# When lane X may begin an output: from the fifth step of a block instead of the third

## The chip, the cores and the metric

The kernel runs on one NeuronCore of a Trainium2 chip. The metric is the device time of one launch in microseconds (us). The kernel before took 5182.59 us as the median of three runs, which lay between 5178.62 and 5191.08 us.

The engines are named as in the profile: PE is TensorE's matmuls, PEld its weight loads, DVE is VectorE, ACT is ScalarE, POOL is GpSimd, SP is SyncE, which here issues all DMAs of the main loop.

## What is computed

An image batch of shape (4, 128, 64, 64) goes through two layers. Cut to what matters:

```python
# layer 0, on x of shape (B=4, C=128, 64, 64), with a residual
xn = layernorm(group_norm(x))                      # over channels
h  = gelu(layernorm(depthwise_conv3x3(xn)))        # then a 1x1 convolution fc2
y  = layernorm(xn + fc2(h))
m  = mamba(y in 4 chunks of 32 channels) + skip * y   # selective scan over 4096 pixels
x  = x + proj(layernorm(xn + m))
# layer 1, on tokens t of shape (4, 4096, 128)
t = t + attention(layernorm(t))                    # 4 heads of 32, all 4096 keys
t = t + top2_of_8_experts(layernorm(t))            # softmax router, 128x128 experts
```

Inside `mamba`, each of 64 channels and 16 states per chunk runs `h = dA * h + dBu` over the pixels, and `y = sum over states of h * C`. Everything is fp32.

## The kernel before

**Blocks and units.** The 4096 pixels of a batch are cut into 8 blocks of 512, so there are 32 blocks, numbered here 0 to 31 (batch = number divided by 8). A block is scanned in 16 units: two halves of the channels, times eight pairs of states. One unit is one `TENSOR_TENSOR_SCAN` of 128 x 1025 on DVE, with a multiply before it (`h<-rows,du`) and one after it (`hc<-rows,h`), eight transposing matmuls that sum `hc` over the states (`y<-ident,hc`), and two exponentials on ACT (`da`).

**Steps.** One loop (`while` after line 1340) runs over steps, called `slot` in the code. Two steps make a unit, so a block is 32 steps and the 32 blocks end at `END` = 1024. A step's place in its block is `slot % 32`; "the third step" is the one with number 2. In each step the program issues, in this order: the loads of rows for a later unit, the decays of the next unit (ACT), in even steps the multiply before the scan, then the second half-step of lane X, one group of attention (4 matmuls `sc`, 2 exponentials `pT`), the scan (even) or the multiply after it (odd), the first half-step of lane Y, the summing transposes, the second half-step of lane Y, the eight matmuls `av` of the attention group of the step before, and the first half-step of lane X. Every engine keeps this order: `queued` (line 406) ties each instruction to the one before it on its engine, which is also why nearly all lines of the profile read L406.

**Lanes.** All work that is neither scan nor attention goes through two lanes, each a queue of tasks written as generators. One half-step is one `yield`. A lane runs one task to its end before it takes the next.

- Lane Y prepares blocks: `in` (the inputs of one channel half: projections, Silu, softplus; 3 steps), `y0` (first norm of a later block; 5 steps), `xn` (convolution, gelu, fc2 and two norms for the next block; 13 steps). In most blocks the order is `in` (from step 3), `y0` (from 6), `xn` (from 11; its convolution taps, 1.5 us of DVE per step, in steps 11 to 15), `in` of the next block (from 24). In blocks 14, 22 and 30 there is no `y0` after the first `in`, so `xn` runs from step 6.
- Lane X finishes blocks. `closed(b, i)` (line 793; 18 half-steps, 9 steps) takes a scanned block through the output projection, the last norm, and the attention's keys, queries and values. When its last half-step is done, `("closed", b, i)` is in `done`. `finished(b, qb, lane)` (line 1032; 30 half-steps, 15 steps; the task is called `out`) takes a block of 512 queries whose attention is complete through the projection (`aT`, `acc`), the router with its top-2 choice (`pr`, `top1`, `pick1`, `both`), and the experts (`share`, `res`). Its half-steps 0 to 19 are loads, projection and router; the eight experts come in half-steps 20 to 28.

**How lane X picks.** When the second channel half of a block is summed, in step 3 of the next block, `summed_up` (line 778) puts `closed` at the front of lane X's queue. An `out` task is put at the end of the queue when its attention is complete. `advance` (line 1254) takes the first task of the queue, with one condition for `out`: before step `END + 4` it is begun only in a window of steps of the block. A task that runs is never interrupted: where an `out` was begun in step 2, `closed` of that block waits until it ends in step 17.

**Attention.** A batch has 256 groups: for each of 4 pairs of query blocks and 4 heads, 32 key tiles in groups of two. `RUNS` (line 903) orders them so that parts whose blocks are closed come first; `ready` (line 908) checks this. The generator gives one group per step, or none where the next part's blocks aren't closed yet. Lane Y takes `out` tasks too once its own queue is empty, from step `END` on, but never a `closed`.

**Buffers.** Each lane has one PSUM bank for its work (`ps_X`, `ps_Y`); a matmul group is written in the first half-step and read in the second. Lane Y's `in` also uses `ps_X` inside a step. `rows` has 4 buffers, `hc` 2, `pT` 4, `sc` 2, lane X's temporaries 6.

Of the kernel before, what the change touches and what calls it, by code (L numbers as in the profile page):

```python
# [24 lines left out]
NST = 16  # L25
# [11 lines left out]
def conv_mamba_attn_moe_kernel(ctx: ExitStack, tc: tile.TileContext, t: dict):  # L37
# [1216 lines left out]
    def advance(lane, second):  # L1254

        if inside[lane] != second:
            return False
        while True:
            if lane not in running:

                tasks = lanes[lane] if lanes[lane] or slot < END else lanes["X"]
                if tasks and lane == "Y" and tasks[0][0][0] == "closed":
                    return False
                if not tasks or not all(k in done for k in tasks[0][2]):
                    return False

                if (
                    tasks[0][0][0] == "out" and slot < END + 4
                    and not 2 <= slot % (2 * NST) < NST + 2
                ):  # L1270
                    return False
                key, stages, _ = tasks.popleft()
                running[lane] = key, stages(lane) if callable(stages) else stages
            key, stages = running[lane]
            try:
                next(stages)
                inside[lane] = not second
                return True
            except StopIteration:
                assert not second  # L1280
                done.add(key)
                del running[lane]

    def until(key):
        while key not in done:
            flush()
            count = len(done)
            moved = [
                advance(*half) for half in (("X", True), ("Y", False), ("Y", True), ("X", False))
            ]  # L1290
            assert any(moved) or len(done) > count, key
            if ("y0", *blocks[1]) in done:
                next(weights, None)
# [49 lines left out]
    h_of, slot = {}, 0  # L1343
# [18 lines left out]
    while (  # L1362
# [16 lines left out]
        if summing:  # L1379
            summed_up(*summing)  # L1380
            summing = None
        advance("X", True)
        group = next(groups, None)
        if group:
# [3 lines left out]
        if unit and odd:  # L1388
            hc = read(h, rows.pop((at, 1)))
            late = 2 * (unit[3] == 0)  # L1390
            due.append((slot + 1 + late, unit, 0, hc[:, 0, :], False))
            due.append((slot + 2, unit, 1, hc[:, 1, :], ends(unit)))
        advance("Y", False)
        while closing and closing[0][0] <= slot:
            summing = turned_back(*closing.popleft()[1:])
# [133 lines left out]
```

## Time and profile before

| what | value |
|---|---|
| median of three runs | 5182.59 us |
| the profiled execution's own time | 5183.13 us |
| its span, first to last instruction | 5180.9 us |
| start of the first scan | 77.8 us |
| start of the last scan (unit 511) | 4570.1 us |
| closing of the last block begins (DVE `cm<-xn,w_skip`) | 4653.8 us |
| first `out`'s loads are issued | 1299.2 us |
| `acc<-ps_X,acc`: outputs in lane X | 27 |
| `acc<-ps_Y,acc`: outputs in lane Y, the first at 4594.5 us | 5 |
| scan on DVE, 512 times | 2353 ns each |
| exponential `pT` on ACT, 2048 times | 1022 ns each |
| table load on ACT, 319 times | 1283 ns each |

How to read it: the start of the scan of unit 16k is the start of block k on DVE, so a block's length is the time from one such scan to the sixteenth after it. Blocks 11, 13, 19, 21 and 27 last 143.5, 142.2, 143.6, 143.5 and 143.5 us. Blocks 14, 22 and 30 last 159.6, 163.4 and 158.9 us. Blocks 7 and 17, in which lane X only closes a block, last 133.5 and 138.9 us. After the last block only attention and outputs remain, some 600 us.

In lists of waits and groups, a name like `ps_X<-ident,bothX` is output, then inputs; "PE ps_X <- DVE bothX" is a wait of PE, before a matmul into `ps_X`, for DVE's write of `bothX`.

### The profile page before, as it was taken

What the parts mean: (1) busy time and instruction counts of PE and PEld (TensorE: products, weight loads), DVE (VectorE), ACT (ScalarE), POOL (GpSimd) and SP (SyncE); (2) the same over time, 40 slices, a digit from 0 to 9 for tenths busy, and PEclk for the clock granted to TensorE, in tenths of its full rate; (3) what the DMA queues carried; (4) which work ended last, traced back from release to release, by engine and by line L of the source; (5) the groups of instructions that cost most, each with busy time, mean ns of one, the idle gap of its engine ahead of it and who ended that gap; (6) DMA issues with size and microseconds to landing.
All of it is one profiled execution on the core that took longest, in us unless ns stands there. A gap on an engine that the chain in (4) does not pass through costs nothing.

```text
span 5180.9 us, 62597 instructions
## 1 busy us (share of the span) xinstructions
PE 4710.1 (91%) x20684; PEld 2321.9 (45%) x20684; DVE 3835.8 (74%) x5780; ACT 3745.7 (72%) x5700; POOL 423.1 (8%) x483
## 2 busy tenths in 40 slices
PE   4567898999999998899999999999999999999997
PEld 2334444444444444444444444444444444443443
DVE  6987767877778887878788887888788877751332
ACT  4556777787787787688888787788777787656543
POOL 1111111100000000101000000000000001000000
PEclk7778999999999999899999999999999999999998
DMA  3556667677666766767766766777766666754542
GB/s 127 183 186 212 205 212 253 233 239 243 229 224 225 239 227 234 242 230 258 252 228 227 238 229 231 258 231 255 265 227 233 221 230 221 262 179 156 184 134 72
DMA packets 451693, 1131.70 MB, mean 218 GB/s; under 512 B 51858, under 2 KB 135331, under 8 KB 451363
## 3 DMA queue, kind: packets, MB, share of 16 engines
q1 hardware_dynamic: 447296, 1125.96, 64.3%
q8 instruction: 166, 2.72, 0.2%
q10 hardware_dynamic: 4066, 1.67, 0.1%
q14 instruction: 165, 1.34, 0.1%
HBM read 967.22 MB, written 143.39 MB: 214 GB/s over the span
## 4 chain that ended last, share of the span: by engine, by line
PE 59%; DVE 19%; ACT 10%; DMA 6%; issue 4%; POOL 2%; SPq 1%; DVEq 0%; ACTq 0%; POOLq 0%
PE av L406 25%; PE sc L406 14%; PE ps_X L406 9%; DVE h L406 6%; PE ps_Y L406 6%; PE y L406 5%; ACT pT L406 3%; ACT L406 2%; DVE hc L406 2%; DMA ks<-kd 2%; ACT xt L406 1%; DVE stX L406 1%; DVE du L406 1%; DMA rows<-bcd 1%; DVE cm L406 1%
## 5 line engine op out<-in xcount | busy, mean ns | idle before, releaser
L406 ACT ACTIVATE pT<-sc 128x1024 f32<-128x1024 f32 x2048 | 1984.3, 1022 | 934.3 <-PE sc L406 932.8
L406 PE MATMUL av<-pT,v 128*64 128x512 f32 x8192 | 2002.8, 610 | 10.8 <-DVE avs L406 10.8
L406 PE MATMUL sc<-qs,ks 128*128 128x512 f32 x4096 | 1302.7, 437 | 75.9 <-ACT pT L406 39.4
L406 DVE TENSOR_TENSOR_SCAN h<-da,state,h 128x1025 f32<-128x1025 f32 x512 | 1204.5, 2353 | 96.6 <-ACT h L406 62.8
L406 PEld LDWEIGHTS sc<-qs,ks 128*128 128x128 f32 x4096 | 703.1, 190 | 812.7 <-ACT pT L406 273.2
L406 PEld LDWEIGHTS av<-pT,v 128*64 128x64 f32 x8192 | 500.4, 137 | 845.7 <-issue 816.7
L406 ACT ACTIVATE da<-delta,amat 128x512 f32<-128x512 f32 x1024 | 742.9, 730 | 1.9
L406 PE MATMUL y<-ident,hc 128*128 128x128 f32 x4096 | 626.2, 284 | 64.6 <-DVE hc L406 64.6
L406 DVE TENSOR_TENSOR hc<-rows,h 128x1024 f32<-128x1024 f32 x512 | 624.6, 1220 | 15.3 <-PE y L406 5.4
L406 DVE TENSOR_TENSOR h<-rows,du 128x1024 f32<-128x1024 f32 x512 | 623.9, 1218 | 13.0 <-DMA rows<-bcd 8.5
L406 PEld LDWEIGHTS y<-ident,hc 128*128 128x128 f32 x4096 | 524.2, 147 | 229.0 <-issue 80.8
L406 ACT ACT_TABLE_LOAD x319 | 409.3, 1283 | 19.5 <-DVE zs L406 14.3
L406 POOL TENSOR_TENSOR rsX<-rsX,mhalf 128x4 f32<-128x4 f32 x92 | 203.7, 2214 | 2504.4 <-DVE rsX L406 2420.4
L406 POOL TENSOR_TENSOR rsY<-rsY,mhalf 128x4 f32<-128x4 f32 x100 | 130.7, 1307 | 2072.5 <-DVE shiftY L406 1561.5
L406 DVE TENSOR_TENSOR avs<-av,prev 128x512 f32<-128x512 f32 x96 | 66.2, 689 | 256.7 <-PE av L406 235.0
L406 PE MATMUL ps_X<-share,w_ew 128*128 128x512 f32 x432 | 213.9, 617 | 9.1 <-DVE share L406 8.8
L406 ACT ACTIVATE xt<-ps_Y,shiftY,rsY 128x128 f32<-128x128 f32 x380 | 143.6, 468 | 81.7 <-POOL shiftY L406 73.8
L406 DVE TENSOR_TENSOR share<-share,xf 128x1024 f32<-128x1024 f32 x128 | 156.0, 1219 | 16.5 <-DMA share<-sharesX 11.7
L406 ACT COPY state<-h 128x2 f32<-128x2 f32 x448 | 88.8, 198 | 92.0 <-DVE h L406 92.0
L406 DVE SCALAR_TENSOR_TENSOR cm<-y,w_fc1w,cm 128x512 f32<-128x512 f32 x195 | 145.1, 744 | 8.0 <-ACT y L406 4.5
L406 PE MATMUL ps_Y<-pairs,inxc 128*128 128x512 f32 x256 | 132.6, 643 | 15.5 <-DMA pairs<-xn 9.9
L406 PEld LDWEIGHTS ps_X<-share,w_ew 128*128 128x128 f32 x432 | 73.2, 189 | 147.0 <-issue 97.1
(248 smaller groups left out, 3437.2 us busy)
## 6 DMA issues: line engine op xcount, KB each, us to landing
rows<-bcd SPq DMA_DIRECT2D x1024, 512.0 KB
ks<-kd SPq DMA_DIRECT2D x192, 512.0 KB
qs<-qd SPq DMA_DIRECT2D x161, 512.0 KB
share<-sharesX SPq DMA_DIRECT2D x108, 512.0 KB
v<-vd SPq DMA_DIRECT2D x192, 256.0 KB
ks<-kd SPq DMA_DIRECT2D x128, 256.0 KB
avd<-avs SPq DMA_DIRECT2D x96, 256.0 KB
prev<-avd SPq DMA_DIRECT2D x96, 256.0 KB
```

The lines of the kernel that those rows point to most:

```text
L406: return lambda *args, **kw: queued(op(*args, **kw))
```

## The change

```diff
                 if (
                     tasks[0][0][0] == "out" and slot < END + 4
-                    and not 2 <= slot % (2 * NST) < NST + 2
+                    and not 4 <= slot % (2 * NST) < 18
                 ):
                     return False
```

`NST` is 16, so the upper end is 18 in both. The window in which an `out` may begin was steps 2 to 17 of a block and is now steps 4 to 17. `closed` enters the queue in step 3. Nothing is added or removed: the same tasks with the same instructions run, in another order.

## The prediction

> **What bounds the kernel now.** I read the page first: engine shares, then the slices.
>
> ```profile
> PE 4710.1 (91%) x20684; PEld 2321.9 (45%) x20684; DVE 3835.8 (74%) x5780; ACT 3745.7 (72%) x5700; POOL 423.1 (8%) x483
> ...
> PE   4567898999999998899999999999999999999997
> ...
> PEclk7778999999999999899999999999999999999998
> ```
>
> PE is full from the fifth slice to the last; the idle time of its start, before attention has data, is outside the change. So I took PE's idle time block by block. Busy time by windows, each from a block's first scan to the next block's (us, then busy time by engine, PEclk, DMA share, GB/s):
>
> ```profile
> 943.20:1076.70 133.50, 126.94 (x586) 61.89 (x585) 104.46 (x136) 113.15 (x163) 15.48 (x19) 1.00 0.64 213
> 2394.60:2533.50 138.90, 131.44 (x601) 63.96 (x599) 109.75 (x144) 114.32 (x175) 12.12 (x13) 0.99 0.76 259
> 2966.60:3110.10 143.50, 140.05 (x641) 69.47 (x640) 117.74 (x176) 117.70 (x183) 11.68 (x15) 1.00 0.70 241
> 3855.10:3998.60 143.50, 140.05 (x641) 69.48 (x640) 117.75 (x176) 116.86 (x181) 11.60 (x14) 1.00 0.67 222
> 1662.20:1804.20 142.00, 127.53 (x574) 65.59 (x572) 118.11 (x177) 108.12 (x172) 11.60 (x14) 0.95 0.71 236
> 1946.40:2106.10 159.70, 133.39 (x560) 68.14 (x559) 128.20 (x198) 101.63 (x160) 15.11 (x11) 0.86 0.75 256
> 3110.10:3273.50 163.40, 150.90 (x664) 74.33 (x664) 128.60 (x197) 118.26 (x180) 12.95 (x15) 0.96 0.74 259
> 4677.00:4792.00 115.00, 115.00 (x464) 45.15 (x460) 9.23 (x13) 72.28 (x76) 0.00 (x0) 1.00 0.46 157
> ```
>
> These are blocks 7, 17, 21, 27, 12, 14, 22, and a stretch of attention alone at the end. Blocks 21 and 27, with an output begun in step 2 and the closing after it, are PE's work (140.05) plus 3.45 us of idle. Blocks 7 and 17, which close in step 3 and have no output, have less work and more idle: 6.6 and 7.5 us. Blocks 12 and 14 lack attention groups in 5 and 8 steps and PE's clock falls. The end is PE alone.
>
> PE's waits in block 7, then in block 21 (total us, times, longest):
>
> ```profile
> PE sc L406 <- ACT pT L406: 2.7, 6, 1.8
> PE ps_Y L406 <- DVE gn L406: 2.1, 1, 2.1
> PE ps_Y L406 <- ACT xt L406: 1.3, 1, 1.3
> PE ps_Y L406 <- ACT g L406: 0.4, 1, 0.4
> ```
> ```profile
> PE ps_X L406 <- DVE bothX L406: 1.9, 1, 1.9
> PE sc L406 <- ACT pT L406: 0.9, 4, 0.4
> PE ps_X L406 <- DVE lo L406: 0.7, 1, 0.7
> ```
>
> The reader is to see that the order in lane X decides which waits a block has. The 2.1 us for `gn` stands in blocks 5, 7, 8, 9 and 17 alike, all that close first: DVE gets to `gn` behind `tt` and the moments of `closed`.
>
> [...]
>
> **The steps, counted from the code.** `closed` takes 9 steps, `out` 15. Before: `out` 2 to 17, `closed` 17 to 26. After: `closed` 3 to 12, `out` 12 to 27 (12 is inside the window). This turns over blocks 10 to 16 and 18 to 31; block 9's output begins in step 16 in both. 22 outputs begin before `END` in both; 22 in lane X plus 5 there in the tail is the 27 of the profile.
>
> Closing 14 steps sooner feeds attention sooner. Taking `ready` step by step, no group is ready in 5 steps of block 12 and 8 of block 14; after the change in 1 and 0. The other steps without a group are the same. So 891 groups, not 879, are done before `END`; 133, not 145, remain, and the loop has 1182 steps, not 1194. The last closing moves from steps 1041-1050 to 1027-1036, but attention doesn't lack groups there, so this alone gives nothing.
>
> **Part 1, twelve groups out of the tail.** In the stretch of attention alone the chain has `av` x8 of 1.87 us and `sc` x4 of 1.12: 2.99 a group. 12 x 2.99 = -35.9.
>
> **Part 2, the steps that they fill.** Blocks 12 and 13 take 142.0 + 142.2 = 284.2 with the holes; two full ones take 2 x 143.5 = 287.0: +2.8. Blocks 14 and 15 take 301.8; the full pair 22 and 23 takes 163.4 + 139.2 = 302.6: +0.8. Together +3.6: PE's idle time and slow clock are traded for work. Net of parts 1 and 2: -32.3.
>
> **Part 3, the order in the 17 ordinary blocks** (10 to 13, 15, 16, 18 to 21, 23 to 29). PE's work is the same 140.05, so a block changes by its waits and its clock. The waits of the new order, in order of steps, from the blocks that already close first:
> - before `closed` the wait for `pT`: 0.2 in both.
> - `gn` in steps 6 to 7: 2.1. Upstream nothing differs from block 7. Ends 1.5 and 2.1.
> - `pT` after it: 0.4 (blocks 5, 7, 17).
> - `xt` in step 18: 1.3 (block 7) to 1.9 (block 17). DVE binds there: 20.05 of 20.5 us in steps 12 to 17 of block 7. The output now adds before that norm `aT` 0.69, `acc` 0.69 and its moments (1.1 + 0.6 + 0.2), 3.3 us of DVE, and on PE `aT`, `acc`, `rw`, 2.3 us: PE waits about 0.9 longer. I take 2.2; ends 0.5 (PE hides it) and 3.0.
> - `g` in step 19: 0.4; ends 0 and 0.5.
> - `both` in step 19: the top-2 choice is 17 small DVE instructions, 3.5 us. It cost 1.9; here PE has just waited for `xt`, and DVE and PE come about level. I take 0.8; ends 0 and 1.9.
> - the second `in`, steps 24 to 26: 1.4 to 1.9 of `pT` in blocks that only close, 0.5 in block 21 after other PE work. The experts[...] now lie there and cover ACT's four table loads of 1.28. I take 0.2; ends 0.2 and 1.4. `lo` 0.7 becomes `res`: 0.2; ends 0 and 0.7.
>
> Sum 0.2 + 2.1 + 0.4 + 2.2 + 0.4 + 0.8 + 0.2 + 0.2 = 6.5 against 3.5: +3.0 a block. Block 9, which closes first and runs an output four steps later, has 6.3 without its waits at the change of batch. What is relieved, DVE 20.19 of 20.30 us in steps 12 to 15 of block 21 (taps beside experts), wasn't PE's wait: 0 gained there.
> Loads: `aT`, `inv` and `acc` are now issued on SP behind `qd<-hi,lo` (2 x 512 KB) and ahead of `vd`, two steps (some 9 us) before use[...]. 0; ends 0 and 1.0. Clock: block 17 lost 1% of 138.9, block 7 nothing: +0.5; ends 0 and 0.8.
> 17 x (3.0 + 0.5) = +59.5. All upper ends together give +7.7 waits a block, all lower -0.7; they won't meet, and I use +0.3 to +5 for the range.
>
> **Part 4, blocks 14, 22, 30.** Taps lie beside `closed` (steps 6 and 7: 4.8 scan + 3.0 taps + 5.0 moments and `tt` = 12.8 us of DVE for 8 of PE, about 4.5 of wait), but the 4.1 for `bothX` shrinks, and experts meet the group norm's statistics. +2 each, ends -2 and +6: +6.
>
> **Sum.** -35.9 + 3.6 + 59.5 + 6 = +33.2 on the profiled execution's 5183.13, which lies 0.5 above the median: 5216, as a median 5215.
>
> **Rivals.**
> 1. Faster: the output's PE work in steps 12 to 27 (some 9.5 us: 140 less 130 to 131) covers `xt`, `both` and `pT`, and only `gn` replaces `bothX`. For: those waits are largest where PE has least to do. Against: DVE, not PE, is later there. Place: steps 16 to 27. Waits +0, parts 1 and 2 alone: 5182.6 - 32.3 = 5150. It decides once a block adds under (32.3 - 15.5)/17 = 1.0 us.
> 2. No change: half of the waits are covered, 1.9 a block: 17 x 1.9 = 32.3, 5183. For: the two parts are of one size. Against: needs them to meet.
> 3. Much slower: late `aT` stalls DVE with all behind it, and PE's clock falls often: 17 x (4.5 + 0.7) + 18 - 32.3 = +74, 5257. Against: DMA share is 0.7 in such blocks.
>
> **How the numbers follow.** Forecast 0.45, rival 1 0.25, rival 2 0.20, rival 3 0.10. 0.3% (15.5 us) is about what a measurement of this kernel can tell. Faster 0.25, same 0.20, slower 0.55. The forecast's own range is 17 x (1.3 + 0.3) - 32.3 = -5 to 17 x (4.5 + 0.5) - 32.3 + 6 = +59: 5177 to 5241. To hold eight in ten it reaches down over most of rival 1 and a little up: 5145 to 5248.
>
> **What would show it.** Right: the last scan some 65 to 70 us later; 891 groups before it ends; ordinary blocks near 147 us with `gn` 2.1 and `xt` about 2; the tail 36 shorter. Wrong: ordinary blocks at or under 144.5 (rival 1), or DVE waiting for `inv` in every block (rival 3).

## The result, and the profile after

The changed kernel takes 5220.88 us as the median of six runs (5215.53 to 5227.74), against 5186.3 us of the kernel before in the same comparison (5178.62 to 5195.01): a ratio of 1.0066, with a 95% interval of 1.0053 to 1.0079. The change costs 35 us. The profiled executions last 5219.3 and 5180.9 us from the first instruction to the last.

The page of the kernel after: busy time of each engine, and the slices for PE and its clock.

```profile
PE 4721.6 (90%) x20684; PEld 2323.0 (45%) x20684; DVE 3835.8 (73%) x5780; ACT 3739.5 (72%) x5700; POOL 466.7 (9%) x483
...
PE   4567898999999999999999999999999999999997
...
PEclk7778999999999999999999999999999999999998
```

The instructions are the same in number on every engine. The dip of before's 16th and 17th slices (8 and 8, and a clock of 8 in the second) is gone: PE's holes in block 14 are filled. And yet the kernel is longer, so time must have come in elsewhere, in pieces too small for a slice of 130 us.

Busy time by windows after: blocks 14 and 21, then all that follows the start of the last scan. Columns as before: length, then busy time (and count) of PE, PEld, DVE, ACT, POOL, then PEclk, DMA share, GB/s.

```profile
1974.60:2129.50 154.90, 143.08 (x642) 71.09 (x643) 127.46 (x197) 113.61 (x173) 13.22 (x11) 0.99 0.79 270
3010.10:3162.10 152.00, 144.52 (x660) 71.06 (x662) 118.62 (x178) 120.53 (x188) 14.73 (x15) 1.00 0.68 229
4641.40:5219.30 577.90, 533.53 (x2110) 229.00 (x2108) 171.63 (x466) 280.06 (x313) 12.29 (x13) 0.95 0.42 139
```

The last scan starts at 4641.4 us, not at 4570.1: 71.3 later. From there to the end it is 577.9 us, not 610.8: 32.9 back. PE's clock in block 14 is 0.99, not 0.86. (A window that is cut by DVE's scans also holds what PE was behind at the cut; block 21 shows 660 matmuls. So I cut by PE below.)

From PE's first summing matmul of a block (`y<-ident,hc`) to that of the next, by the records of both traces. "Idle" is PE's idle time; "half clock" is half the length of the stretches with a granted clock under 1, an estimate of the time they cost: the granted clock is 0.50 in all 50 of them before and in all 58 after, and the eight `av` of a group take 3.34 us where all but the first 0.4 lies in one (after, at 2758.95 us), and 1.94 at a clock of 1.00 (after, at 1897.12 us). Where PE idles inside such a stretch the two overlap, as in block 14 before.

| stretch (us) | before | after | change | idle | half clock |
|---|---|---|---|---|---|
| start and blocks 0 to 9, same order in both | 1394.6 | 1403.2 | +8.6 | +1.6 | +6.9 |
| ordinary 10 to 13, 15, 16 | 861.5 | 888.8 | +27.3 | 32.7 to 41.9 | 8.5 to 11.9 |
| block 14 | 157.0 | 155.0 | -2.0 | 26.3 to 11.8 | 22.2 to 1.7 |
| block 17 | 138.9 | 144.4 | +5.5 | 7.5 to 10.8 | 1.7 to 3.4 |
| ordinary 18 to 21, 23 to 29 | 1598.7 | 1630.4 | +31.7 | 57.7 to 81.4 | 10.2 to 15.4 |
| blocks 22 and 30 | 314.4 | 311.3 | -3.1 | 23.9 to 22.8 | 11.9 to 8.5 |
| block 31 and all after | 715.8 | 686.3 | -29.5 | 44.5 to 48.3 | 21.6 to 26.8 |

The first row is no effect: five kernels of the experiments (E1, E2, E5, E6, E8) have the same order there too and take 1398.8 to 1403.7 us for it. So a row of one profiled execution can be off by several us. The rest is the ledger of the change: what the ordinary blocks lose is more than what the tail gives back.

The names in the waits below: `gn` is the group-normed input of lane Y's `y0`, `cm` the sum of the convolution taps in `xn` and `g` the gelu behind it, `xt` the result of a norm. In lane X, `tt` is the sum ahead of the norm of `closed`, `hi` and `lo` are the two parts in which it stores keys and queries, and `aT` and `inv` are what an output loads first (the attention sum and what it is multiplied by). `ks` are attention's keys.

PE's waits over the whole execution, before and then after (total us, times, longest):

```profile
PE ps_X L406 <- DVE bothX L406: 45.5, 25, 4.1
...
PE ps_Y L406 <- DVE gn L406: 35.6, 14, 4.8
PE sc L406 <- DMA ks<-kd: 35.4, 16, 5.1
...
PE ps_X L406 <- DVE lo L406: 19.9, 23, 2.6
...
PE ps_Y L406 <- ACT g L406: 7.3, 10, 1.7
PE ps_Y L406 <- DVE cm L406: 3.6, 4, 1.1
...
PE ps_X L406 <- DVE aT L406: 2.5, 3, 2.0
```
```profile
PE ps_Y L406 <- DVE gn L406: 62.8, 27, 4.8
...
PE sc L406 <- DMA ks<-kd: 50.2, 18, 4.9
...
PE ps_X L406 <- DVE aT L406: 23.9, 15, 3.0
PE ps_Y L406 <- DVE cm L406: 23.6, 21, 1.6
...
PE ps_Y L406 <- ACT g L406: 21.6, 30, 1.7
...
PE ps_X L406 <- DVE bothX L406: 8.0, 10, 2.5
...
PE ps_X L406 <- DVE lo L406: 3.5, 5, 1.7
```

This pair is the whole case. The waits of the old order, `bothX` and `lo`, fall by 37.5 + 16.4 = 53.9 us. Five others rise: `gn` by 27.2 (13 more of them), `aT` by 21.4, `cm` by 20.0, the key loads `ks<-kd` by 14.8, `g` by 14.3: 97.7 together. None is long. In one ordinary block, number 13, after (1825.7 to 1974.6 us):

```profile
PE ps_Y L406 <- DVE gn L406: 2.1, 1, 2.1
PE ps_Y L406 <- DVE cm L406: 1.6, 1, 1.6
PE ps_Y L406 <- ACT g L406: 1.1, 1, 1.1
PE ps_X L406 <- DVE aT L406: 1.0, 1, 1.0
PE sc L406 <- ACT pT L406: 0.6, 3, 0.2
```

`aT` and `cm` stand close together, as DVE's timeline of the same block after shows (start, length, instruction, and in brackets the idle time ahead of it):

```profile
1893.91 0.69 DVE L406 TENSOR_TENSOR aT<-aT,inv 128x512 f32<-128x512 f32 x1 [1.57 <-issue]
1894.52 2.35 DVE L406 TENSOR_TENSOR_SCAN h<-da,state,h 128x1025 f32<-128x1025 f32 x1
1896.79 1.51 DVE L406 SCALAR_TENSOR_TENSOR cm<-y,w_fc1w,cm 128x512 f32<-128x512 f32 x2
1898.22 0.68 DVE L406 TENSOR_TENSOR acc<-ps_X,acc 128x512 f32<-128x512 f32 x1
1898.94 0.87 DVE L406 BATCH_NORM_STATS2 stX<-acc 128x6 f32<-128x128 f32 x4
...
1900.20 1.22 DVE L406 TENSOR_TENSOR hc<-rows,h 128x1024 f32<-128x1024 f32 x1
1901.34 0.74 DVE L406 SCALAR_TENSOR_TENSOR cm<-y,w_fc1w,cm 128x512 f32<-128x512 f32 x1
```

The multiply of `aT` starts 11.3 us after its load was issued (1882.57 us), with 1.57 us of idle time ahead of it. The profile names no cause here; in block 21 it names the loads (DVE's waits after, 3010.1 to 3162.1 us):

```profile
DVE aT L406 <- DMA inv<-inverse: 2.0, 1, 2.0
```

Behind the multiply in block 13 stand the scan, two convolution taps, `acc` with its moments and the multiply `hc`, and only then the last tap, for which lane Y's next matmul waits. Two causes are possible for that wait: the late `aT`, which pushes everything back, or the output's `acc` and moments, which stand ahead of the tap even when `aT` is in time. E9 below decides it: it is mostly the second.

### The profile page after: what moved, and what is told of

The parts are those of the page before. It is cut to its first block, busy times and chain, and to the rows that moved or that the text cites. A ratio compares the mean times of both kernels' runs of the same rounds, so it can differ in the third digit from the quotient of the medians.

```text
span 5219.3 us, 62556 instructions
## 1 busy us (share of the span) xinstructions
PE 4721.6 (90%) x20684; PEld 2323.0 (45%) x20684; DVE 3835.8 (73%) x5780; ACT 3739.5 (72%) x5700; POOL 466.7 (9%) x483
## 4 chain that ended last, share of the span: by engine, by line
PE 57%; DVE 17%; ACT 9%; DMA 9%; issue 4%; POOL 3%; SPq 1%; DVEq 0%; ACTq 0%; POOLq 0%
PE av L406 24%; PE sc L406 13%; PE ps_X L406 8%; PE ps_Y L406 6%; PE y L406 5%; DVE h L406 5%; ACT pT L406 3%; DMA ks<-kd 3%; DMA inv<-inverse 2%; DVE hc L406 2%; ACT L406 2%; POOL rsX L406 2%; ACT xt L406 1%; DVE stX L406 1%; DMA rows<-bcd 1%
## 5 line engine op out<-in xcount | busy, mean ns | idle before, releaser
L406 PE MATMUL y<-ident,hc 128*128 128x128 f32 x4096 | 626.5, 284 | 60.1 <-DVE hc L406 60.1
L406 ACT ACT_TABLE_LOAD x319 | 409.3, 1283 | 19.5 <-DVE zs L406 14.3
L406 DVE TENSOR_TENSOR res<-res,ps_X 128x512 f32<-128x512 f32 x108 | 74.0, 685 | 225.7 <-PE ps_X L406 225.4
L406 DVE TENSOR_TENSOR cm<-ps_X,cm 128x512 f32<-128x512 f32 x32 | 22.1, 692 | 178.0 <-PE ps_X L406 178.0
L406 PE MATMUL ps_Y<-pairs,inxc 128*128 128x512 f32 x256 | 132.9, 645 | 21.4 <-DMA pairs<-xn 15.8
```

The lines of the kernel that those rows point to most:

```text
L406: return lambda *args, **kw: queued(op(*args, **kw))
```

## The experiments

Each kernel is the one before or the one after with the edit shown, and each ratio is against the kernel before in the same comparison.

**Which blocks pay, and is the late closing worth anything?** The first kernel (E1) opens the window at step 4 from block 18 on only, where no attention is missing; the second (E2) only after the last block.

```diff
-                    and not 4 <= slot % (2 * NST) < 18
+                    and not (4 if slot >= 18 * 2 * NST else 2) <= slot % (2 * NST) < 18
```

> The new window holds from block 18 on alone; blocks 10 to 17 keep the old one. No attention group moves: 879 are done before the last block ends, as before. My theory (the order in lane X costs some 3 us of PE's waits in each ordinary block, and only the groups that fill the holes of blocks 12 and 14 give anything back): 11 ordinary blocks turned over with no gain in return, +29 to +40 us on before, so 5215 to 5226. Rival (the loss sits in the steps that were filled, in blocks 12 to 15): as before, 5186 +- 8.

Measured: 5214.57 us, 1.0062 [1.0049, 1.0075], 33 us above before. The 11 ordinary blocks of 18 to 29 take 1634.4 us (before 1598.7), those of 10 to 16 take 862.7 (861.5).

```diff
+                    and not (4 if slot >= END else 2) <= slot % (2 * NST) < 18
```

> The new window holds from step 1024 on alone: the last block is closed 14 steps sooner, everything earlier is as before. My theory (attention doesn't lack groups there, the end is a count of groups at 2.99 us): no change, within 8 us of before. Rival (the tail of the changed kernel is shorter because the last closing comes sooner): 20 to 36 us under before.

Measured: 5186.46 us, 1.0002 [0.9994, 1.0011]. The last closing begins at 4588.8 us there, not at 4653.8. So the order in ordinary blocks costs by itself, block after block, and closing the last block 65 us sooner gains nothing by itself.

**Can the waits be moved away?** The first of these (E3) puts one step more (two half-steps) between DVE's multiply of `gn` and PE's transposes of it, so that PE asks later; lane Y's convolution behind it moves on by a step as well. The next (E4) gives the output's loads one step more.

```diff
 # first_norm
         vector.tensor_scalar(gn, gn, gm, gr, ALU.subtract, ALU.mult)
+        yield
+        yield
         yield
         ps = transposed(lane, by_tile(gn))
```

> The changed kernel, with two more half-steps between the multiply of gn on DVE and its transposes on PE: PE asks for it one step later, and the convolution runs one step later, so its last tap no longer stands behind acc and its moments. My theory (waits of PE that are in its queue's way are lost time): the 2.1 us for gn go in 22 blocks (-46) and the 1.6 for cm in some 14 (-22), less what appears anew: 40 to 65 us under the changed kernel, 5156 to 5181. Rival (DVE and ACT bind the block, PE's waits only show it, and they come back elsewhere): within 15 us of the changed kernel's 5221.

Measured: 5243.58 us, 1.0116 [1.01, 1.0132]: about 26 us slower than after, by the two ratios (0.0050 of 5183). Both theories missed. PE's waits of that kernel over the whole execution:

```profile
PE y L406 <- DVE hc L406: 113.3, 54, 9.2
...
PE ps_X L406 <- DVE bothX L406: 22.3, 24, 2.5
...
PE ps_Y L406 <- DVE gn L406: 3.0, 2, 2.2
```

`gn` falls from 62.8 to 3.0, and the summing matmuls' wait for `hc` rises from 60.1 to 113.3 (34 more of them), `bothX` from 8.0 to 22.3. The new wait for `hc` is 1.6 us in most ordinary blocks and lies in steps 6 and 7, where that for `gn` lay. What is late there is DVE as a whole, behind `tt` and the moments of `closed`; whichever matmul needs DVE first has the wait. These three sums rise by 7.7 us together; where the rest of the 26 us lies was not taken apart.

```diff
 # finished, after its three loads
         yield
         yield
         yield
+        yield
+        yield
         vector.tensor_mul(aT, aT, inv)
```

> The changed kernel, with two more half-steps between an output's loads and its first multiply aT: the loads have one step more to land, and acc moves one step on, off the last tap and beside the moments of lane Y. My theory (DVE waits for aT and inv, which are issued behind the writes of qd, and PE for DVE): the 0.7 to 3.0 us for aT go in 17 blocks (-27) and the 1.6 for cm in 14 (-22), but a wait for xt of 1 to 2 us appears (+25): 10 to 40 us under the changed kernel. Rival (the aT wait is DVE's load, not the DMA): the aT wait stays, within 10 us of 5221.

Measured: 5234.87 us, 1.0099 [1.0083, 1.0114], about 17 us slower than after; again both theories missed. `aT` falls from 23.9 to 3.0 and `cm` from 23.6 to 4.2, since `acc` and its moments now come after the last tap; but ACT's `xt` rises from 66.2 to 98.4 (45 waits for 20), `share` from 1.3 to 16.5, and the half clock in the ordinary blocks from 18 on costs 30.7 us, not 15.4. (E1, with lane X's order as after in these blocks and the same idle time, 81.2 and 81.4 us, has 25.6, so much of that step can be chance.) A wait that is taken out here comes back in other places.

If DVE's piece of `tt` and moments is the cause of `gn`, cutting it must help `gn`. Between the addition and the norm of `closed` (E7):

```diff
 # closed, after tt is sent to be kept
+        yield
+        yield
         # the norm of tt follows
```

> The changed kernel, with the moments of tt one step after tt in the closing, which so takes 10 steps; the output begins in step 13. My theory (PE's wait of 2.1 us for gn is DVE's 3.3 us of tt and moments in one half-step, bare because PE has no backlog after the first inputs): DVE's piece halves and the wait falls to 0.8 or less; the time changes less, since the output is then placed as in e4_out: 5205 to 5240. Rival (gn waits for its load or for POOL): the wait stays at 2.1.

Measured: 5302.57 us, 1.0237 [1.0213, 1.0262]. PE's waits of that kernel in its block 13:

```profile
PE sc L406 <- ACT pT L406: 2.2, 6, 0.6
PE ps_X L406 <- DVE aT L406: 2.0, 1, 2.0
...
PE ps_Y L406 <- DVE gn L406: 0.3, 1, 0.3
```

`gn` falls from 2.1 to 0.3, and to 0.8 or less in every block from 5 on: that part of the cause is shown. The time is far over what was expected. The output now starts a step later, `aT` and `pT` are late, and in the ordinary blocks from 18 on PE idles 100.8 us (after 81.4) and loses 39.3 to the half clock (15.4). Which of these brought the others was not taken apart.

Last, the output far from the taps: it may begin only in steps 16 and 17 (E8).

```diff
-                    and not 4 <= slot % (2 * NST) < 18
+                    and not 16 <= slot % (2 * NST) < 18
```

> An output may begin in steps 16 and 17 alone: the block is closed in steps 3 to 12, lane X rests for four steps, the output runs from 16 to 31. The groups are as in the changed kernel (891, 1182 steps). My theory (the wait for aT is the loads beside the writes of qd and vd): the aT wait falls under 0.5, g and cm stay about 1 each, pT returns beside the second inputs (+1.4), gn stays 2.1: ordinary blocks have 5.5 to 6.5 of waits, the time is 5205 to 5225. Rival (most of the changed kernel's loss is the output beside the taps): 5185 to 5200.

Measured: 5224.37 us, 1.0073 [1.0056, 1.0089], the same loss as after. `cm` falls to 10.4 us and `aT` to 10.2, `pT` rises from 38.8 to 63.7 and `xt` to 86.3; `gn` stays at 62.8. So the output's place beside the taps is not what costs most. The wait for `aT` falls by half; at most 0.5 a block was expected, and four blocks have 1.6 to 2.2. DVE waits even longer for the outputs' loads, 80.1 us in 20 waits over the execution (45.6 in 14 after), though they are now issued long after `closed`'s writes. In block 13 the multiply starts 10.2 us after the issue, with 2.9 us of idle time ahead of it. So the closing's writes are not needed to make these loads late. The kernel before has 60.7 us in 20 such waits of DVE, and there PE's own waits for `aT` are 2.5 us in all: a late load need not cost PE any time.

**Keep the filled holes, pay in fewer blocks.** With closing first only where it feeds attention and in a few more blocks. The first list, of six, is E5. The second, of eight (E6), is the shortest found, by counting steps, that still does all twelve groups more before `END`; the six do ten.

```diff
+                    and not (
+                        4 if slot // (2 * NST) in (12, 14, 16, 22, 24, 30) or slot >= END else 2
+                    ) <= slot % (2 * NST) < 18
```

> The new window holds in blocks 12, 14, 16, 22, 24, 30 and from step 1024 on; all other blocks keep the old order. Counted from the code: 889 groups are done before the last block ends, 10 more than before, and the loop has 1184 steps. My theory (gain: 10 x 2.99 = 30 us, less 3 for the steps filled; cost: 3 ordinary blocks at 3 to 4 us, while 14, 22 and 30 change by -2 to 0): 5181 - 27 + 11 - 3, so 15 to 25 us under before, 5156 to 5168. Rival (turning a block over costs through its neighbours, so few turned blocks cost as much as many): within 8 us of before or above.

Measured: 5169.07 us, 0.9965 [0.9952, 0.9977], as expected.

```diff
+                        4 if slot // (2 * NST) in (12, 13, 14, 16, 20, 22, 24, 30) or slot >= END else 2
```

> As e5_six, with blocks 13 and 20 turned over too: these eight are the fewest with which all 12 groups move (891 before the end, 1182 steps). My theory: two more groups (-6) for two more ordinary blocks (+7): within 6 us of e5_six, so 12 to 25 us under before. Rival: as for e5_six, at or above before.

Measured: 5167.72 us, 0.9964 [0.9951, 0.9978], as expected and no better than the six. Block 31 and all after take 682.6 us there (after 686.3, before 715.8) and the ordinary blocks from 18 on 1594.7 (before 1598.7): the gain of the change without most of its price.

**Take away the late load.** The three loads of the next output are issued when `closed` begins, nine steps before the output; `aT` and `inv` go into one of the experts' three `share` buffers instead of two of lane X's temporaries. On the kernel after this is E9, on E6 it is E10, on the kernel before E11.

```diff
 # closed, at its start
+        if lanes["X"] and lanes["X"][0][0][0] == "out" and slot < END:
+            _, ob, oq = lanes["X"][0][0]
+            w = side.tile([P, 2, BLK], F32, name="share", bufs=3)
+            loaded[ob, oq] = loads(ob, oq, w[:, 0, :], w[:, 1, :])
 # finished
+        acc, aT, inv = loaded.pop((b, qb), None) or loads(b, qb, tmp(lane, "aT"), tmp(lane, "inv"))
```

> The changed kernel, with the loads of aT, inv and acc of the next output issued at the start of the closing (step 3) instead of at its end (step 12), into a buffer of the experts' shares that is free then. My theory (DVE waits for aT because its loads queue behind the closing's writes to qd and vd, with the DMA engines full): the waits for aT go from every block, 17 x 1.6 = 27 us of PE, some of it coming back as xt or both: 10 to 30 us under the changed kernel, 5190 to 5211. Rival (the waits for aT only show that DVE is late): within 8 us of 5221.

Measured: 5165.44 us, 0.9963 [0.9949, 0.9976]: about 53 us below after by the two ratios, where 10 to 30 were expected. PE's waits of that kernel over the whole execution:

```profile
PE ps_Y L406 <- DVE gn L406: 62.9, 27, 4.8
...
PE sc L406 <- DMA ks<-kd: 32.5, 17, 6.4
PE ps_Y L406 <- DVE cm L406: 22.8, 24, 1.4
...
PE ps_X L406 <- DVE aT L406: 2.9, 2, 2.1
```

`gn` and `cm` stay. `aT` loses 21.0 us, and `ks<-kd`, attention's own key loads, loses 17.7: they had been late too. That `cm` stays settles the question above: in block 13 it is 1.0 us, where it was 1.6 with the late `aT`, so most of it is the output's `acc` and moments ahead of the last tap. In the ordinary blocks from 18 on, PE idles 63.2 us (after 81.4) and the half clock costs 6.8 (15.4).

Here is the stretch of block 13 in which the kernel after issued those loads (10 us), and its end, in which DVE and PE came to wait (4 us); columns of the windows as above. First after, then the same steps with the earlier loads, which lie 11.3 us sooner there (`qd<-hi` is issued at 1880.06 us in the one and at 1868.79 in the other):

```profile
1878.00:1888.00 10.00, 10.00 (x51) 5.64 (x50) 8.96 (x11) 7.23 (x13) 0.00 (x0) 1.00 1.01 354
1890.00:1894.00 4.00, 3.65 (x18) 1.66 (x16) 2.39 (x4) 2.75 (x5) 0.00 (x0) 1.00 0.98 291
```
```profile
1866.70:1876.70 10.00, 10.00 (x50) 5.61 (x49) 8.98 (x11) 7.24 (x13) 0.00 (x0) 1.00 1.04 388
1878.70:1882.70 4.00, 4.00 (x21) 2.05 (x20) 3.96 (x5) 2.78 (x5) 0.00 (x0) 1.00 0.72 207
```

In the ten microseconds the DMA engines are as full without the output's loads (1.04) as with them (1.01); in the four at the end their share is 0.72 and not 0.98, and PE and DVE are busy (4.00 and 3.96 us) where they waited after. So the earlier loads don't empty this stretch: they keep `aT` and `inv` out of it, and it ends sooner. After, `aT`, `inv` and `acc` (256 KB each) go out between `qd<-hi,lo`, `rows` and `vd` (512 KB each). In this stretch `aT`'s multiply started 11.3 us after the issue of its load.

With the eight blocks (E10):

> e6_eight with the same earlier loads. My theory: 8 blocks have the wait, so 4 to 12 us under e6_eight, 5156 to 5164, 0.4 to 0.6% under before. Rival: as e6_eight.

Measured: 5133.17 us, 0.9897 [0.9881, 0.9913], more than expected: 1.0% faster than before, and 1.7% than after (0.9897 / 1.0066 = 0.983). It is 35 us below E6, where 4 to 12 were expected; where the rest comes from was not taken apart. Here 38 loads of `acc` are issued for 32 outputs: six are loaded twice, since two closings can follow each other with the same output next.

With the old order (E11):

> The kernel before with the earlier loads alone: in its order an output's loads are issued at the start of the closing before it (step 17), if it is in the queue by then. My theory (in the old order DVE's late aT falls in the stretch in which ACT binds, so PE hardly waits for it, 0.4 us in all; what the loads gain there is the clear way for other loads at the changes of batch): 0 to 20 us under before, so that half or more of e10_eight_ahead's gain is the filled holes. Rival (the earlier loads make most of e10_eight_ahead's 51 us in any order): 30 us or more under before.

Measured: 5189.85 us, 1.0017 [1.0009, 1.0025], 9 us slower, which neither theory had. DVE's waits for these loads fall from 60.7 to 39.8 us, but PE hardly waited for `aT` in this order (2.5 us in all), so there is nothing to gain; what costs the 9 us is open. The earlier loads and the closing that comes first need each other.

## Why the prediction was right, and where its terms were off

The forecast's mechanism held, and its size: the holes are filled, the tail is shorter, and the ordinary blocks pay more than that. That the sum came so close, 33 us forecast and 35 measured, is luck in part: in the profiled pair the tail gave back 6.4 less than expected and block 17 cost 5.5 that were in no term, while blocks 14, 22 and 30 came out 11.1 better. Term by term, in PE's time (the table above):

- **The tail**, -35.9 expected. It is -29.5: PE's work there falls by 38.5, but idle and half-clock time grow by 9.0. Why they grow is not shown: E2, whose tail has all 145 groups, already has 30.2 us of half clock there, against 21.6 before and 26.8 after.
- **Ordinary blocks**, +3.5 each. The 11 from 18 on rise by 31.7, which is 2.9 each: +2.2 of idle, +0.5 of half clock and +0.3 of PE's own time. Those of 10 to 16, with block 14 and the groups that fill the holes, change by 27.3 - 2.0 = 25.3 (21.0 + 3.6 of part 2 + 2 of part 4 = 26.6 expected). The sum of this term is right. Its level was not: the 3.5 of waits came from blocks 21 and 27, but the 11 blocks had 5.2 us of idle time each on average before, and have 7.4 after. E1, which changes only blocks from 18 on, shows that this term needs neither hole nor tail.
- **The single waits** that made up the 6.5 of a block were right in one and wrong in most. `gn` is 2.1, exactly as read from block 7, and E7 shows its cause. `xt`, expected at 2.2, and `bothX`, at 0.8, are not in block 13's list at all. In their place stand `cm` at 1.6 and `aT` at 1.0 to 3.0, and `g` is 1.1, not 0.4. Block 13 sums to 6.4, beside the 6.5 forecast, by errors that cancel: a fortunate sum, and the blocks vary (block 16: `aT` 1.9). The experts' matmuls, which were to cover ACT's four table loads (5.1 us), start 0.43 us apart (most of them) or 0.53 in the trace of before, so 16 of them take some 7 us.
- **Loads**: the mis-sized term is "0; ends 0 and 1.0". PE waited 23.9 us for `aT`, in 15 waits of up to 3.0. The prediction took "two steps (some 9 us)" as enough and a DMA share of 0.7 as an argument against late loads. That share is a block's mean; in the ten microseconds that count it is 1.01, and the multiply started 11.3 us after the issue. E9 and E4 show it: loads that come sooner, or a multiply that comes later, take `aT` away.
- **`ks<-kd`** had no term. It costs 14.8 us more, of which 3.4 in block 17, which I had as unchanged (+5.5). E9 takes it back to 32.5, but in block 17 it leaves 3.4.
- **Blocks 14, 22 and 30**, +2 each: they are shorter by 2.0, 1.9 and 1.2 in this pair. That is no sure gain, since block 14 in the old order takes 157.0 us before, but 153.2 in E1 and 154.2 in E2. The loss that was expected isn't there: in block 14 the waits for `bothX` (3.6), `lo` (4.6) and `gmv` (6.0) fell to 0.4, 0.5 and 2.4.
- **The rivals**: the covered block (rival 1) didn't come; ordinary blocks lay near 148 us. Nor did the even trade (rival 2): a block adds 2.9 us and not 1.9. In "much slower" (rival 3) the late `aT` was real, but a block had to add 5.2. Its sign, DVE waiting for `inv` in every block, came nearly: DVE idles ahead of `aT`'s multiply, 0.3 to 3.5 us, in 19 of the 20 blocks from 10 to 30 that begin an output after closing. But the kernel before has such waits too, 60.7 us in all, so it was no sign of what PE loses.

What stays open: why E3, E4 and E7, which each took out the wait they were aimed at, all came out slower; how much of E9's 53 us is the key loads, the clock, and `aT` each, since all three fell in one edit; and whether the other buffers that E9 uses for `aT` and `inv` have a part in it. E11, which has them too and gains nothing, speaks against that in the old order alone.

## What to carry to other kernels

Here every engine works through a fixed order of many short pieces, and the reordering was paid in short waits that no share or slice showed (five kinds rose by 97.7 us together, the longest single one 4.9); compare the two lists of waits over the whole execution, wait by wait, with their counts. A load that is "early enough" by a mean DMA share has to be priced in the window where it is issued: in block 13 after, the share is 0.68 over the block and 1.01 in those ten microseconds. When two orders each have a stretch in which they are better, choose for each block: the order that fed attention in eight blocks, with its loads earlier, beat both.

## What had not been expected of the hardware

Idle gaps of PE went with a second loss, on top of their own length. In the ordinary blocks from 18 on, seven of the thirteen traces have 46.8 to 63.2 us of idle time and lose 3.4 to 13.7 us more to the half clock; the other six have 81.1 to 100.8 and lose 15.4 to 39.3. One pair says less than the thirteen, as the 25.6 of E1 and the 15.4 of after at the same idle time show. The gaps were short: after has nine half-clock stretches in these blocks, and the longest gap that begins in the 7 us ahead of one is 2.1 to 3.7 us, in six of the nine at most 2.94. The traces show that idle time and half clock rise together; what lowers the clock they do not show.
